# Wider moving operands in two of the three product groups of a split-precision attention kernel

## The chip, the cores and the metric

The kernel runs on one core of one Trainium2 chip. A time is the device time of one execution in microseconds (us). Ten executions of the kernel before the change lie between 2486.03 and 2490.31 us, with a median of 2488.53 us. A profile is taken from one more execution: it records the start and the duration of every instruction on TensorE (matmuls as PE, weight loads as PEld), VectorE (DVE), ScalarE (ACT), GpSimd (POOL) and SyncE (SP), and of every DMA packet.

## The reference

For each of four images, x has 4096 positions (64 x 64) with 256 channels. Cut to what matters:

```python
q = jnp.einsum('bwhc,cd->bwhd', x, Wq) + bq      # 128 channels
k = jnp.einsum('bwhc,cd->bwhd', x, Wk) + bk      # 128 channels
v = jnp.einsum('bwhc,cd->bwhd', x, Wv) + bv      # 256 channels
pq, pk, pv = q.reshape(B, -1, N), k.reshape(B, -1, N), v.reshape(B, -1, N)   # N = 4096
energy = jnp.einsum('bcn,bcm->bnm', pq, pk)
attention = jax.nn.softmax(energy, axis=-1)
out = jnp.einsum('bcm,bnm->bcn', pv, attention)
return gamma * out.reshape(B, W, H, C) + x
```

So it is a softmax attention over 4096 positions, with a contraction over 128 for the energies and over 4096 for the output. All data is float32.

## The kernel before, in words

**Precision by splitting.** TensorE works here on operands of the type fp32r, a shorter form of float32 that is stored in four bytes. To keep the accuracy of float32, each operand is split into parts: a rounded upper part, and one or two rests. The energies are three products of such parts for each block (line 325): two are accumulated in one PSUM tile, `sa`, and one goes into another, `sb`. ScalarE takes the exponential of both (line 329), VectorE multiplies the two results (`join`, line 339) and so has the unnormalised attention weights x. Then `upper` (line 344, ScalarE) makes h from x, and `halves` (lines 350 and 353, VectorE) makes l and d from x and h.

**The attention products.** `attend` (line 358) multiplies h, l and d with the three parts vh, vl and vd of v. h times vh and l times vl accumulate in the PSUM tiles a0 and a1 (one for each 128 of the 256 output positions of a block, index j); d times vd goes into the tile bb. The result is put together later as (1 + E) times a plus bb (`whole`, line 405).

**The column of ones.** The tiles vh and vl have a pitch of VC = C + 64 = 320 columns for each of the NM = 32 blocks of v: 256 of v, and then 2 that are set to one at the start (line 220); the rest is unused. As h and l are each multiplied with a one in column 256, column 256 of a0 and a1 holds the sum of the attention weights, which is the softmax's denominator. `sums` (line 390) reads that one column, C : C + 1. The second column of ones is read by no one. The products of h and l are so 258 columns wide (`right[:, m, : out_.shape[1]]`, line 378), those of d 256.

**Blocks and order.** An image's output positions are cut into NG = 16 blocks of 256 (g), and the 4096 positions that are summed over into NU = 8 units of 512 (t). One step u is one pair (g, t): 128 steps for an image, 512 in all. The order on every engine is written out by hand (`manual_schedule`, line 200). In each step TensorE gets 12 energy matmuls for the unit three steps ahead (LOOK = 3, lines 523 to 525: two halves k of six matmuls), and then the 24 matmuls of `attend` for this step: eight with h, eight with l, eight with d, in each eight j = 0, 1 outside and i = 0 to 3 inside. Each matmul has a weight load of its own, of 128 x 128. The loops of `attend` before the change are

```python
for left, right in ((h, vh), (l, vl), (d, vd)):
    for j in range(NJ):
        out_ = bb[:, j, :] if left is d else acc[j]
        for i in range(4):
            m = 2 * t + i // 2 + NI * (i % 2)
```

After the last unit of a block ScalarE copies bb out (line 385) and VectorE takes the sums and a0, a1 (lines 390 and 405). The next block's first h product has to wait for that, since a0 and a1 have one buffer each. Other matmuls are those of the projections of q, k and v (lines 136 and 157), and transposes (lines 123, 421, 462). The PSUM tiles a0 and a1 share their places with the projections' tiles of 2 x 256 float32 (line 225), which sets the size of these places.

Of the kernel before, what the change touches and what calls it, by code (L numbers as in the profile page):

```python
# [9 lines left out]
F32 = mybir.dt.float32  # L10
# [10 lines left out]
def kernel(  # L21
# [36 lines left out]
    nc = tc.nc  # L58
    B, W, H, C = x.shape
    P = 128  # L60
    N = W * H
    C2 = C // 2
    NM = N // P
# [23 lines left out]
    ones = const.tile([P, P], F32, name="ones")  # L87
# [111 lines left out]
    with ExitStack() as fast:  # L199
# [12 lines left out]
        ps_o = pool("ps_o", 1, space=PSUM)  # L212
# [3 lines left out]
        vh = qkv.tile([P, NM, VC], F32R, tag="vh", name="vh")  # L216
        vl = qkv.tile([P, NM, VC], F32R, tag="vl", name="vl")
        vd = qkv.tile([P, NM, C], F32R, tag="vd", name="vd")
        for t in (vh, vl):
            nc.scalar.copy(t[:, :, C : C + 2], ones[:, : 2 * NM].rearrange("p (m t) -> p m t", t=2))  # L220

        images, qd, kf, units, loads, now = [], {}, {}, {}, {}, {}

# [134 lines left out]
        def attend(b, u):  # L358

            g, t = divmod(u, NU)  # L360
            if t == 0:
                now["acc"] = [
                    ps_o.tile([P, C + 2], F32, tag=f"a{j}", name=f"a{j}_{b}_{g}")
                    for j in range(NJ)
                ]
                now["bb"] = ps_o.tile([P, NJ, C], F32, tag="bb", name=f"bb_{b}_{g}")
            h, l, d = units[b, u]
            acc, bb = now["acc"], now["bb"]
            for left, right in ((h, vh), (l, vl), (d, vd)):
                for j in range(NJ):  # L370
                    out_ = bb[:, j, :] if left is d else acc[j]
                    for i in range(4):
                        m = 2 * t + i // 2 + NI * (i % 2)

                        nc.tensor.matmul(  # L375
                            out_,
                            left[:, i, j * P : (j + 1) * P],
                            right[:, m, : out_.shape[1]],
                            start=(t == i == 0 and (left is h or left is d and j == 0)),
                            stop=(t == NU - 1 and i == 3 and left is not h),  # L380
                            skip_group_check=True,
                        )
            if t == NU - 1 and (b, g) != (B - 1, NG - 1):
                now["o"] = work.tile([P, NJ, C], F32, tag="o", name=f"o_{b}_{g}")
                nc.scalar.copy(now["o"], bb)  # L385
# [101 lines left out]
        for b in range(B):  # L487
# [20 lines left out]
            for u in range(STEPS):  # L508
                g, t = divmod(u, NU)
# [26 lines left out]
                if u in (1, 3):  # L536
                    halve_v(b, NI - 2 + u // 2)
                attend(b, u)
                if (b, u) == (B - 1, STEPS - 1):
                    finish_last(b, g, loads.pop((b, "x", g)))  # L540
# [13 lines left out]
    with tc.If(nc.values_load(again[0:1, 0:1]) > 0), ExitStack() as general:  # L554
# [7 lines left out]
        ps_o = pool("go", 1, space=PSUM)  # L562
        for b in range(B):
# [16 lines left out]
            for g in range(NG):  # L580
                ps = []
                mx = work.tile([P, 2, NB], F32, tag="mx", name=f"gmx_{b}_{g}")
                for t in range(NP):
# [9 lines left out]
                    p = ppool.tile([P, 2, NB], F32, tag="p", name=f"gp_{b}_{g}_{t}")  # L593
# [7 lines left out]
                for j in range(NJ):  # L601
# [17 lines left out]
                acc = [  # L619
                    ps_o.tile([P, NB], F32, tag=f"o{s}", name=f"go{s}_{b}_{g}")  # L620
                    for s in range(2)
                ]
# [60 lines left out]
```

## Time and profile before

| | before |
|---|---|
| median of 10 runs | 2488.53 us (2486.03 to 2490.31) |
| the profiled execution's own time | 2486.82 us |
| its span, first to last instruction | 2484.9 us |
| granted TensorE clock, mean | 0.999 |
| PE busy / weight loads busy | 2469.5 us (99%) / 2423.3 us (98%), 19982 of each |
| DVE busy / ACT busy / POOL busy | 2103.4 us (85%) / 1805.6 us (73%) / 424.4 us (17%) |
| DMA | 498.92 MB, mean 201 GB/s |

The page gives a group of instructions by its line, engine, operation, tiles and shapes, with how often it ran, its busy time in all, the mean duration of one, and the idle time of the engine just before it. Matmuls are pipelined: the duration of one matmul runs from its start until its last result, and the next one starts long before that. For a stream of matmuls the number that adds up to time is therefore not the duration but the distance from one start to the next. A row of the timeline with "x8" stands for eight matmuls of one kind in a row; the start of the next row less the start of this one, divided by eight, is that distance.

### The profile page before, as it was taken

The page shows a single profiled execution, that of the slowest core. Times are in us where ns is not written, and L with a number is a line of the kernel's source. Part 1 is how long each engine was busy: PE and PEld are TensorE (multiplying, and loading weights), DVE is VectorE, ACT ScalarE, POOL GpSimd, SP SyncE. Part 2 cuts the span into 40 slices and gives each one's busy share as a digit, 9 for nine tenths or more (in the row PEclk, how much of TensorE's full clock was granted, in tenths as well). Part 3 has the DMA queues.
Part 4 walks back from the last instruction along what each step waited for, and adds up shares of the span by engine and source line. Part 5 has one row for each costly group of instructions (what it writes and reads, how often), then busy time and mean ns, then how long its engine had stood idle before and what let it go on. Part 6 is the DMA issues. An engine that isn't in the chain of part 4 may idle for free.

```text
span 2484.9 us, 50133 instructions
## 1 busy us (share of the span) xinstructions
PE 2469.5 (99%) x19982; PEld 2423.3 (98%) x19982; DVE 2103.4 (85%) x2440; ACT 1805.6 (73%) x3138; POOL 424.4 (17%) x780
## 2 busy tenths in 40 slices
PE   9999999999999999999999999999999999999998
PEld 8999999999899999999989999999998999999998
DVE  5888888888688888888869888888886988888887
ACT  5777777776677777777667777777766777777775
POOL 4211111111411111111041111111114111111110
PEclk9999999999999999999999999999999999999999
DMA  7666666664766666666476666666648666666663
GB/s 227 219 199 207 205 202 200 199 209 156 229 211 192 211 208 200 204 191 211 148 241 217 200 193 212 202 208 198 194 150 250 214 201 199 201 204 208 200 195 115
DMA packets 137408, 498.92 MB, mean 201 GB/s; under 512 B 15536, under 2 KB 57264, under 8 KB 137168
## 3 DMA queue, kind: packets, MB, share of 16 engines
q0 software_dynamic: 92320, 453.17, 58.0%
q1 hardware_dynamic: 44304, 42.22, 5.7%
q8 instruction: 160, 2.62, 0.4%
q14 instruction: 80, 0.66, 0.1%
q10 hardware_dynamic: 544, 0.26, 0.0%
HBM read 445.25 MB, written 50.33 MB: 199 GB/s over the span
## 4 chain that ended last, share of the span: by engine, by line


## 5 line engine op out<-in xcount | busy, mean ns | idle before, releaser
L329 ACT ACTIVATE x<-sa 128x512 f32<-128x512 f32 x1024 | 608.3, 594 | 391.6 <-PE sa L325 363.7
L339 DVE TENSOR_TENSOR x<-x,y 128x1024 f32<-128x1024 f32 x512 | 625.4, 1221 | 146.5 <-ACT y L329 146.5
L325 PE MATMUL sa<-q,k 128*128 128x256 f32 x4096 | 740.9, 279 | 1.9 <-ACT x L329 1.8
L350 DVE TENSOR_TENSOR l<-x,h 128x1024 fp32r<-128x1024 f32 x512 | 623.8, 1218 | 3.9 <-DMA kf<-f 3.9
L353 DVE SCALAR_TENSOR_TENSOR d<-h,x 128x1024 fp32r<-128x1024 f32 x512 | 623.8, 1218 | 0.0
L325 PEld LDWEIGHTS sa<-q,k 128*128 128x128 f32 x4096 | 619.3, 188 | 4.1 <-ACT x L329 3.5
L329 ACT ACTIVATE y<-sb 128x512 f32<-128x512 f32 x1024 | 613.9, 600 | 0.0
L375 PE MATMUL a<-vh,h 128*128 128x258 f32 x4096 | 580.7, 284 | 0.0
L375 PE MATMUL a<-vl,l 128*128 128x258 f32 x4096 | 577.6, 284 | 0.0
L344 ACT ACTIVATE h<-x 128x1024 fp32r<-128x1024 f32 x512 | 543.4, 1061 | 45.0 <-DVE x L339 41.0
L325 PE MATMUL sb<-q,k 128*128 128x256 f32 x2048 | 575.0, 281 | 0.0
L375 PE MATMUL bb<-vd,d 128*128 128x256 f32 x4096 | 555.9, 278 | 0.0
L309 POOL DMA_DIRECT2D k<-kf x512 | 279.6, 546 | 1475.0 <-PE sb L325 1456.5
L375 PEld LDWEIGHTS a<-vl,l 128*128 128x128 f32 x4096 | 530.5, 191 | 0.0
L375 PEld LDWEIGHTS a<-vh,h 128*128 128x128 f32 x4096 | 524.8, 190 | 2.1
L375 PEld LDWEIGHTS bb<-vd,d 128*128 128x128 f32 x4096 | 514.2, 189 | 0.0
L325 PEld LDWEIGHTS sb<-q,k 128*128 128x128 f32 x2048 | 384.9, 188 | 10.4 <-ACT y L329 1.7
L136 PE MATMUL qk<-wqk_sb,xts 128*128 128x256 f32 x512 | 121.3, 380 | 0.0
L405 DVE SCALAR_TENSOR_TENSOR o<-a,o 128x256 f32<-128x256 f32 x126 | 47.6, 420 | 86.8 <-ACT o L385 86.8
L157 PE MATMUL v<-xts,wv_sb 128*128 128x256 f32 x512 | 120.3, 379 | 0.0
L157 PEld LDWEIGHTS v<-xts,wv_sb 128*128 128x128 f32 x512 | 97.3, 190 | 13.2
L413 ACT ACTIVATE o<-o,r 128x256 f32<-128x256 f32 x126 | 57.4, 502 | 72.4 <-DVE r L396 72.4
(54 smaller groups left out, 928.0 us busy)
## 6 DMA issues: line engine op xcount, KB each, us to landing
k<-kf POOLq DMA_DIRECT2D x512, 768.0 KB, 4.8
x<-in_x_dram SPq DMA_DIRECT2D x128, 256.0 KB, 3.7
kf<-f POOLq DMA_DIRECT2D x64, 384.0 KB, 3.6
out_dram<-x POOLq DMA_DIRECT2D x63, 256.0 KB, 2.5
qd<-qks POOLq DMA_DIRECT2D x128, 64.0 KB, 2.9
qr<-qd SPq DMA_DIRECT2D x64, 128.0 KB, 5.0
wv_sb<-in_L_conv_Wv_dram POOLq DMA_DIRECT2D x1, 256.0 KB, 7.4
out_dram<-x SPq DMA_DIRECT2D x1, 256.0 KB, 3.9
```

The lines of the kernel that those rows point to most:

```text
L136: nc.tensor.matmul(qk[:, s, :], self.xt[i][:, k, s, :], wqk_sb[:, k, :], start=(k == 0), stop=(k == KC - 1),)
L157: nc.tensor.matmul(vp[:, eh, :], wv_sb[:, k, eh * P : (eh + 1) * P], self.xt[i][:, k].rearrange("p s a -> p (s a)"), start=(k == 0), stop= ...
L309: nc.gpsimd.dma_start(t.rearrange("p (i s) f d -> p i s (f d)", s=2), kf[b, u % NU])
L325: nc.tensor.matmul(to[:, i], kt[:, 2 * k + i, f, :], q[:, f], start=first, stop=last)
L329: nc.scalar.activation(to[:, 2 * k : 2 * k + 2, :], sp.rearrange("p i j d -> p i (j d)"), AF.Exp, scale=scale,)
L339: nc.vector.tensor_tensor(x, x, y, ALU.mult)
L344: nc.scalar.activation(h, units[b, u], AF.Identity, scale=UPPER)
L350: nc.vector.tensor_tensor(l, x, h.bitcast(F32), ALU.subtract)
L353: nc.vector.scalar_tensor_tensor(d, h.bitcast(F32), 1.0 + E, x, ALU.mult, ALU.subtract)
L375: nc.tensor.matmul(out_, left[:, i, j * P : (j + 1) * P], right[:, m, : out_.shape[1]], start=(t == i == 0 and (left is h or left is d and ...
L405: nc.vector.scalar_tensor_tensor(o[:, j, :], a[:, :C], 1.0 + E, o[:, j, :], ALU.mult, ALU.add)
L413: nc.scalar.activation(o[:, j, :], o[:, j, :], AF.Identity, scale=r[:, j : j + 1])
```

## The change

The products of h take 260 columns of vh, those of l take 264 columns of vl, and those of d take 256 as before. Columns 256 to 263 of vh and vl are all set to one at the start, where two columns were set before. The PSUM tiles a0 and a1 get C + 8 columns. The pitch VC of vh and vl stays at 320. Column 256 is read for the sums, as before; the columns behind it are read by no one.

```diff
         for t in (vh, vl):
-            nc.scalar.copy(t[:, :, C : C + 2], ones[:, : 2 * NM].rearrange("p (m t) -> p m t", t=2))
+            nc.scalar.copy(t[:, :, C : C + 8], ones[:, :1].unsqueeze(1).to_broadcast([P, NM, 8]))
...
-                    ps_o.tile([P, C + 2], F32, tag=f"a{j}", name=f"a{j}_{b}_{g}")
+                    ps_o.tile([P, C + 8], F32, tag=f"a{j}", name=f"a{j}_{b}_{g}")
...
-            for left, right in ((h, vh), (l, vl), (d, vd)):
+            for left, right, wide in ((h, vh, C + 4), (l, vl, C + 8), (d, vd, C)):
                 for j in range(NJ):
-                    out_ = bb[:, j, :] if left is d else acc[j]
+                    out_ = bb[:, j, :] if left is d else acc[j][:, :wide]
...
-                            right[:, m, : out_.shape[1]],
+                            right[:, m, :wide],
```

## The prediction

> **What bounds the kernel now.** I read the engines' shares first.
>
> ```profile
> PE   2469.5 (99%) x19982; PEld 2423.3 (98%) x19982; DVE 2103.4 (85%) x2440; ACT 1805.6 (73%) x3138; POOL 424.4 (17%) x780
> ...
> PEclk9999999999999999999999999999999999999999
> ```
>
> TensorE is busy from end to end at its full clock. A share of 99% alone proves little for pipelined matmuls, so the waits come second. This is TensorE's own list of waits, in full:
>
> ```profile
> PE wp L197 <- POOL ident masks.py:199: 2.4, 1, 2.4
> PE sa L325 <- ACT x L329: 1.8, 6, 0.3
> PE xt L123 <- DMA x<-in_x_dram: 1.8, 1, 1.8
> PE ot L462 <- DVE o L457: 1.1, 1, 1.1
> ```
>
> Some 7 us of 2484.9 are waits for others, most of them at the start and the end. The chain of waits on the page is empty, and none is needed: a step lasts as long as its 36 matmuls take to start one after the other. So a change in the distance between starts goes into the time almost one to one. The third view is one step in TensorE's timeline (start, us, kind):
>
> ```profile
> 1016.85 0.39 PE L325 MATMUL sa<-q,k 128*128 128x256 f32 x2
> ...
> 1018.21 1.12 PE L375 MATMUL a<-vh,h 128*128 128x258 f32 x8
> 1019.18 1.13 PE L375 MATMUL a<-vl,l 128*128 128x258 f32 x8
> 1020.14 1.08 PE L375 MATMUL bb<-vd,d 128*128 128x256 f32 x8
> 1021.06 0.39 PE L325 MATMUL sa<-q,k 128*128 128x256 f32 x2
> ```
>
> The 12 energy matmuls take 1018.21 - 1016.85 = 1.36 us, 113 ns each. Eight h products take 0.97 us and eight l products 0.96 us, 120 to 121 ns each. Eight d products, 256 wide like the energies, take 0.92 us, 115 ns each. Two columns more cost 7 ns. That can't be the two columns' own streaming: 113 ns for 256 is 0.44 ns a column at most.
>
> The start times of single matmuls in the trace show it finer (timestamps of 1 ns, averaged over repeats). In 340 of the 512 steps the distances are the same. Energies run at 113.33 ns. Then, from h's first product on, each to the next start: 114.2, 119.2, 125.0, 119.2, 120.0, 123.3, 120.0, 121.7; l's: 118.3, 119.2, 125.0, 119.2, 120.0, 123.3, 120.0, 121.7; d's: 117.5, 116.7, 115.8, 114.2, and 113.3 again. Three things are to be seen. **First**, the first 258-wide product costs 114.2, that is 0.83 ns more than a 256-wide one, or 0.42 ns a column. **Second**, what follows holds a stall over that, 6.67 ns on average (120.83 - 114.17), in a pattern that repeats every eight products. It repeats by its own count and not by i and j: in other steps the 125 falls on another product. **Third**, d's first four products, of 256, still pay 10.8 ns in all. So the stall is a state of the stream, a rhythm that is lost and found again, more than a price of each product. Other rhythms in the trace are 120.00 exactly for 258 (72 steps), and 117.78 for 256 in 67 runs of more than ten energies and d products.
>
> **The change, part by part.** Over all 512 steps the means are 121.4 ns for h (971.6 for eight), 120.7 for l (965.7) and 115.7 for d (925.3). There are 4096 products of each kind.
>
> *Streaming of more columns.* h gets 2 more and l gets 6 more. At 0.42 ns a column from the first-product row that is +0.83 ns x 4096 = +3.4 us for h and +2.5 ns x 4096 = +10.2 us for l, +13.7 us together. Nothing hides this: it is on TensorE.
>
> *The stall.* No product of 260 or 264 columns is in the trace. The bounds for what remains of the 6.67 ns stall are 0 (the first product; the energies) and, above, a stall as now or more. Nearest rows: 4.44 ns for 256 in its second rhythm (117.78 - 113.33), 5.83 ns for 258 at 120.00. 6.67 is the largest steady stall that I find in this trace; a new width shifts the rhythm by another amount per product, and is more likely to land below that than above. I take half, 3.33 ns, for both widths: h would be 113.33 + 4 x 0.42 + 3.33 = 118.3, l 113.33 + 8 x 0.42 + 3.33 = 120.0. Against 120.83 that is -2.5 ns x 4096 = -10.2 us for h and -0.83 ns x 4096 = -3.4 us for l, together -13.6 us. With a stall of 0 it would be -5.8 x 4096 = -23.9 and -4.2 x 4096 = -17.1 us, and d would lose its tail of 10.8 ns x 512 = -5.5 us: -46.5 us. With the stall as now it is +13.7 us. I leave d's tail as it is.
>
> A rule speaks against the change here. The Trainium skill, "TensorE: Matmul & The Clock Gate", section "Back-to-back issue gap", has a warm matmul start N / 2.4 + 2.5 ns after the one before, which estimates 110.0 ns for 258, 110.8 for 260 and 112.5 for 264. By that rule alone the change can only cost, some 13.7 us. The rows say 120.8 for 258 and 113.3 for 256, so something that the rule lacks is at work, and it is larger than what the rule has to say on the added columns.
>
> *The ones.* Two ScalarE copies of 128x64, of 247 and 243 ns at 3.0 us, become 128x256. A ScalarE row of that size and output type takes 420 ns (line 261), so +0.35 us in all. ScalarE then stands idle for 3.04 us until the first transposes are there at 6.45 us; that covers it. Without the cover it would cost 0.35 us.
>
> *Nothing else moves.* The pitch of vh and vl stays 320, so no address in SBUF changes. a0 and a1 keep their places, which the projections' tiles of 2 KB set. `sums` reads the same column. The order of no queue changes.
>
> *What is late next.* If the step of 4.21 us falls to 4.12 (the 46.5 us case), VectorE is next: it is busy for 18.58 us of the stretch from 600 to 620 us, the fuller of the two that I read, which is 3.9 us a step. It stays under TensorE, with little room.
>
> **The sum** is against the profiled execution: 2486.82 - 13.6 = 2473.2 us. The median of the runs is 1.7 us above that execution, so **2475 us** for the median.
>
> **The rivals.**
> (a) *The stall goes almost wholly* because 258 ends on a remainder that the stream can't take in step, and 260 and 264 don't. For it: the first 258-wide product pays nothing, and the period is eight products, in which two columns become sixteen. Against it: a remainder of 4 or 8 in sixteen still shifts. 2488.5 - 46.5 = 2442 us; if only one width profits, about 2455 to 2470.
> (b) *A grid of sixteen columns*: 120.00 less 113.33 is 6.67, sixteen columns at 0.42. If the stream takes 64-byte pieces, 258, 260 and 264 all cost 120.00. The change then doesn't touch the cause. The 440 steps not yet in that rhythm gain 0.83 x 16 ns, 5.9 us; d's eight take 929.6 ns after it and 921.8 in the 340 steps, which takes 3.4 us back. About 2486 us.
> (c) *The other side*: the stall stays as it is, since any width over 256 breaks the step of weight load and matmul, and the added columns stream on top: +13.7 us, 2502 us. For it: 120.83 is just 114.17 plus 6.67, the price of sixteen columns once more, as if one beat were missed per product at any width. It decides as soon as the stall shrinks by less than 1.67 ns, the mean of 0.83 and 2.5.
> (d) *A worse rhythm* than any here, at 125 (the largest distance in the pattern) for both: 4.2 x 8192 = +34 us, 2523 us.
>
> **How the numbers follow.** Forecast, the stall partly gone (2457 to 2483): 0.35. (a): 0.16. (b): 0.13. (c), up to 2512: 0.28. (d): 0.08. About 0.2% (5 us) is what a measurement of this kernel can tell from no change. Faster by more than that: forecast and (a), 0.51. Within: (b), 0.13. Slower: 0.36. The range leaves out (d) and the larger part of (a): 2450 to 2506. Cases of both signs are in it; the likeliest one's own range is 2457 to 2483.
>
> **What would show it.** The start distances in the new trace: h near 118 and l near 120 ns would bear out the forecast, 115.0 and 116.7 rival (a), 120.0 for both (b), 121.7 and 123.3 (c). d's tail tells whether the rhythm is kept: eight d products in 0.91 us, not 0.92. The energies must stay at 113.3, and the waits of TensorE at some 7 us; if they grow, VectorE or ScalarE has become late and the sum is wrong for another reason. It is wrong from the start if the distances of h and l are set by something other than their width.

## The result and the profile after

The changed kernel takes 2497.89 us (median of 8 runs, 2496.82 to 2500.47) against 2488.75 us for the kernel before (28 runs). The ratio is 1.0038, with a 95% interval of 1.0030 to 1.0047: slower by 9 us, where 13.6 us less had been forecast. The profiled execution took 2497.8 us, with a span of 2495.9 us, 11.0 us more than the span before. The engines' shares on its page:

```profile
PE 2480.1 (99%) x19982; PEld 2435.4 (98%) x19982; DVE 2105.0 (84%) x2440; ACT 1806.9 (72%) x3138; POOL 425.7 (17%) x780
```

TensorE's list of waits, in full (who waited, on whom, us in total, times, longest):

```profile
PE wp L197 <- POOL ident masks.py:199: 2.4, 1, 2.4
PE sa L325 <- ACT x L329: 2.0, 7, 0.3
PE xt L123 <- DMA x<-in_x_dram: 1.9, 1, 1.9
PE ot L463 <- DVE o L458: 1.1, 1, 1.1
```

TensorE still waits for others for no more than some 7 us. The list has idle time alone; a gap that the running matmul's own duration of some 280 ns covers is not in it. From the start times, 313 energies before and 310 after have the next start more than 140 ns behind them, some 31 and 30 us over the pace of 113.3 ns, so these gaps did not grow either. No other engine became the bound, and the 11 us are in the products themselves. One step in TensorE's timeline (start, us, kind):

```profile
1026.79 1.12 PE L376 MATMUL a<-vh,h 128*128 128x260 f32 x8
1027.74 1.16 PE L376 MATMUL a<-vl,l 128*128 128x264 f32 x8
1028.73 1.09 PE L376 MATMUL bb<-vd,d 128*128 128x256 f32 x8
1029.66 0.28 PE L325 MATMUL sa<-q,k 128*128 128x256 f32 x1
```

Eight h products take 0.95 us where they took 0.97; eight l products 0.99 where they took 0.96; eight d products, whose width did not change, 0.93 where they took 0.92. The single starts, medians over the 512 steps, each to the next: h 116, 118, 122, 118, 120, 122, 118, 120 ns; l 124, 119, 120, 121, 122, 127, 130, 132; d 115, 119, 120, 118, 118, and then 113. What is to be seen is l: its distances grow to the eighth product.

Added up over all steps from the start times in the two traces, from one matmul's start to the next's:

| us | before | after | change |
|---|---|---|---|
| h | 497.5 | 493.8 | -3.7 |
| l | 494.5 | 509.0 | +14.5 |
| d | 473.8 | 478.1 | +4.3 |
| energies | 732.5 | 728.1 | -4.4 |
| all others | 276.0 | 276.1 | +0.1 |

The energies gain mostly because they run less often in the second pace of 256, the 117.8 ns that the prediction had met: 312 of 6144 have a distance of 116 to 120 ns, 1077 before. At 4.4 ns each that is 3.4 us.

### The profile page after: what moved, and what is told of

It is laid out like the page before. It is cut to its first block, busy times and chain, and to the rows that moved or that the text cites. A ratio compares the mean times of both kernels' runs of the same rounds, so it can differ in the third digit from the quotient of the medians.

```text
span 2495.9 us, 50133 instructions
## 1 busy us (share of the span) xinstructions
PE 2480.1 (99%) x19982; PEld 2435.4 (98%) x19982; DVE 2105.0 (84%) x2440; ACT 1806.9 (72%) x3138; POOL 425.7 (17%) x780
## 4 chain that ended last, share of the span: by engine, by line
## 5 line engine op out<-in xcount | busy, mean ns | idle before, releaser
L376 PE MATMUL a<-vl,l 128*128 128x264 f32 x4096 | 592.2, 287 | 0.0
L376 PE MATMUL a<-vh,h 128*128 128x260 f32 x4096 | 577.3, 283 | 0.0
L376 PEld LDWEIGHTS bb<-vd,d 128*128 128x128 f32 x4096 | 523.8, 189 | 0.0
L157 PE MATMUL v<-xts,wv_sb 128*128 128x256 f32 x512 | 120.3, 379 | 0.0
```

The lines of the kernel that those rows point to most:

```text
L157: nc.tensor.matmul(vp[:, eh, :], wv_sb[:, k, eh * P : (eh + 1) * P], self.xt[i][:, k].rearrange("p s a -> p (s a)"), start=(k == 0), stop= ...
L376: nc.tensor.matmul(out_, left[:, i, j * P : (j + 1) * P], right[:, m, :wide], start=(t == i == 0 and (left is h or left is d and j == 0)), ...
```

## The experiments

Theory 1, from the two traces: each width has its own pace, and 264's is bad. Theory 2: 264 is bad only behind 260. Theory 3: every width over 256 costs the time of 32 columns more than it has, at 0.42 ns a column, rival (c) of the prediction. Ratios are against the kernel before on the same chip, whose median was 2483.35, 2484.93 and 2485.87 us in the three sets of timed runs. The trace of the kernel before belongs to the set with 2488.75 us, so a difference of a few us between a run's trace and that trace need not be the change's. Four programs of products alone were built, each profiled once, with 64 bytes between the moving tile and the weights as the kernel has. The rows of the moving tile have 320 columns as those of vh and vl (384 in the last program), those of the weights 256 as in the kernel in the first program, then 320, 320 and 384. The granted clock is 1.0 in all of the runs below. A column has four bytes; `at` is the column at which the moving operand starts in its row, `shift` that of the weights:

```python
nc.tensor.matmul(out[:, :w], wt[:, i, shift + j*128 : shift + j*128 + 128], mv[:, m, at : at + w], ...)
```

**Streams of one width.**

> Another program, of products alone: runs of 64 products with weights of 128 columns at each of 15 widths from 256 to 320, and of 64 weight columns at six widths, with 24 products of 256 between the runs; no other engine works beside it; its output is not the attention. Theory 1, each width has its own steady pace for a weight load and a product: 256 at 113.3 ns, 258 at 120.0 to 120.9, 260 at 119.5 to 120, 264 at 123 to 125, the same from the eighth product to the last. Theory 2, a grid of sixteen columns: 258 to 272 all at 120.0, 274 to 288 at 126.7. Theory 3, two beats are missed at any width over 256: (width + 32) / 2.4, 121.7 at 260, 123.3 at 264, 126.7 at 272. If the weight load sets the pace, the runs with 64 weight columns go at (width + 16) / 2.4 or less, 114.2 at 258 and 116.7 at 264; if the moving side does, they are as slow as those with 128.

TensorE's timeline; a row of x64 is one width, and its start to the next row's start, divided by 64, is its pace:

```profile
37.98 7.89 PE L58 MATMUL a<-mv,wt 128*128 128x258 f32 x64
45.71 2.89 PE L50 MATMUL sp<-mv,wt 128*128 128x256 f32 x24
48.44 7.84 PE L58 MATMUL a<-mv,wt 128*128 128x260 f32 x64
56.11 2.99 PE L50 MATMUL sp<-mv,wt 128*128 128x256 f32 x24
58.94 8.02 PE L58 MATMUL a<-mv,wt 128*128 128x262 f32 x64
66.80 2.91 PE L50 MATMUL sp<-mv,wt 128*128 128x256 f32 x24
69.54 7.87 PE L58 MATMUL a<-mv,wt 128*128 128x264 f32 x64
77.25 2.91 PE L50 MATMUL sp<-mv,wt 128*128 128x256 f32 x24
```

7.73, 7.67, 7.86 and 7.71 us for 64: 120.8 ns at 258, 119.8 at 260, 122.8 at 262, 120.5 at 264. Over the last 32 products alone, from the start times, the paces are 113.3 (256), 120.8, 120.1 (260), 122.7, 120.0 (264), 123.3 (266), 126.7 (268), 124.5 (270), 123.3 (272) and 133.3 (288). So neither the straight line of theory 3 (121.7, 123.3 and 126.7 at 260, 264 and 272) nor the flat grid of rival (b). And 264 is not slow in the long run: its first products come at 117, 120, 121, 122, 127, 130, 132 and 118 ns, and from the ninth on every one at 120.0. That beginning is the row of l in the changed kernel. No other engine works beside these products, so none is the cause. Theory 1 falls in its own form: what l pays is the **beginning of a run of 264**, and a run of eight is over before the pace is found. Second, the rows of 24 products of 256: after 260 they take 58.94 - 56.11 = 2.83 us, 117.9 each, and after 258 2.73 us, 113.8 each. A run leaves the stream behind it in one pace or the other, and it stays there for all 24. With only 64 weight columns a weight load takes 134 ns in the trace where it took 188 (medians), and the paces are 119.1 (256), 118.7 (258), 120.0 (264) and 124.1 (272): slower at 256, 2 ns faster at 258, the same at 264. A shorter weight load does not take the stall away.

**h and l both 260, both 264, both 256.**

```diff
-            for left, right, wide in ((h, vh, C + 4), (l, vl, C + 8), (d, vd, C)):
+            for left, right, wide in ((h, vh, C + 4), (l, vl, C + 4), (d, vd, C)):   # h260_l260
+            for left, right, wide in ((h, vh, C + 8), (l, vl, C + 8), (d, vd, C)):   # h264_l264
+            for left, right, wide in ((h, vh, C), (l, vl, C), (d, vd, C)):           # h256_l256, sums from ones
```

> h and l both 260 wide. Theory 1 (the price is the width's own): h stays at 964 ns for eight as in the changed kernel, l comes to 955 to 960 in place of 994, d back to some 925 or less: 2478 to 2484 us, faster than 258. Theory 2 (what matters is that h and l have different widths, or how long the off-step run is): l at 960, d as with 258: about 2484. Theory 3 (width + 32 cycles): h and l 121.7, 2495 us.

2493.63 us, ratio 1.0036 (1.0022 to 1.0050). h and l did as theory 1 and 2 said, 963 and 961 ns for eight, and still the kernel is slower: 3303 of the 6144 energies are in the second pace. Theory 1 had expected a time under that of 258. A step:

```profile
1024.75 0.40 PE L325 MATMUL sa<-q,k 128*128 128x256 f32 x2
...
1026.16 1.12 PE L376 MATMUL a<-vh,h 128*128 128x260 f32 x8
1027.12 1.12 PE L376 MATMUL a<-vl,l 128*128 128x260 f32 x8
1028.08 1.07 PE L376 MATMUL bb<-vd,d 128*128 128x256 f32 x8
1028.99 0.39 PE L325 MATMUL sa<-q,k 128*128 128x256 f32 x2
```

Twelve energies take 1.41 us here, 117.5 ns each, without any change to them. In this trace they cost 742.2 us (732.5 before) and d 476.5 (473.8). The 2226 energies more that are in the second pace make up 9.9 us at 4.4 ns each: the loss was moved from the wide products to the narrow ones.

> h and l both 264 wide. Theory 1: h as slow as l, 985 to 995 ns for eight: 2510 to 2515 us. Theory 2 (264 is only slow behind 260): both at 960 to 970: 2485 to 2490. Theory 3: 123.3 ns each, 2509 us.

2498.63 us, ratio 1.0059 (1.0045 to 1.0073). Now it is h that takes 996 ns for eight (118, 120, 121, 123, 127, 130, 132, 118), and l runs at 120.0. So both theories had half: the costly beginning comes once for each run of 264, behind energies of 256 here and behind 260 in the changed kernel. Sixteen of 264 cost less extra than theory 1 had it.

> No column of ones in the products: h and l 256 wide, and the sums are copied from a tile of ones, so the output is not divided by the softmax's denominators. All theories: h, l and d at 113.3 ns, 906 to 910 for eight, so (971.6 + 965.7 + 925.3 - 3 x 908 + waits as before) x 512, some 60 to 70 us less than with 258: 2420 to 2430 us. It is the whole price of the columns over 256. If h, l or d stay above 115 ns, the price is not the width's.

2430.95 us, ratio 0.9788 (0.9773 to 0.9803): 52 us are the whole price of a denominator in the products, of which streaming two columns at 0.42 ns would be 6.8. h took 916.5 ns for eight (with the wait at the start of a block), l 910, d 913. Against the trace before, h, l and d together fell by 63 us, as expected; the energies took 5 us more, as 90 of them have the next start more than 250 ns behind them and not 26.

**One part of the change alone.**

> One part alone: h back at 258, l at 264. If the first seven products of 264 pay for getting into their pace whatever stood before (as in the run of 64 products of 264: 117 to 132 ns, then 120.0), l takes 985 to 995 ns for eight and h 971: 0.5 to 0.8% over the kernel before. If l's price came from following 260, l is at 960 to 966 and the time within 0.2% of before.

2501.60 us, ratio 1.0068 (1.0055 to 1.0082); l 992 ns for eight, h 973, d 936. The price of l did not come from following 260. A step:

```profile
1022.79 1.13 PE L376 MATMUL a<-vh,h 128*128 128x258 f32 x8
1023.76 1.16 PE L376 MATMUL a<-vl,l 128*128 128x264 f32 x8
1024.75 1.10 PE L376 MATMUL bb<-vd,d 128*128 128x256 f32 x8
```

> The other part alone: h at 260, l back at 258. h at 964 ns for eight, l at 960 to 967. If the second pace of 256 (117.8 ns) that follows 260 in the run of products alone decides, d and the energies slow down as in the kernel with 260 for both, unless 258 in between resets it: with the reset 0.1 to 0.3% under the kernel before, without it 0.2 to 0.5% over.

2481.51 us, ratio 0.9989 (0.9980 to 0.9998): h 965 ns, l 966, d 924, and only 398 energies in the second pace. h's part of the change is a gain, small and just clear of no change; l's part is the whole loss.

**The place of the operands.** If the stall is a matter of step and not of columns, something else than the width should move it. Products and weight loads go on side by side: PE was busy for 99% and PEld for 98% of the span before.

> Products alone again, in runs of 64 with 24 products of 256 between; its output is not the attention. Now the widths under 256, the place of the operands and mixed widths. Theory W, the count of columns sets the pace: 256 columns that start 2, 4, 8 or 16 columns into a row of the moving tile go at 113.3 ns as ever, 258 at 120.8 from column 8 or 14 as well, and 258 and 264 keep their 120.8 and 120.0 when the weights start 64, 128 or 192 bytes further. Theory L, pieces of 64 bytes: 256 columns from column 2, 4 or 8 touch 17 pieces and go at 120 or more, from column 16 at 113.3; 258 from column 14 touches 17 and stays at 120.8. Theory B, the two read streams collide in SBUF: the place of the weights moves the pace of 258 and 264 by some ns. Under 256: by width alone (width + 16) / 2.4, 106.7 at 240; if the weight load is the limit, 113.3 at all four. Alternating 258 with 256: if the stall is a lost step that a 256 regains, 114.2 and 113.3, a mean under 115; if not, 117 to 121.

```profile
68.29 7.84 PE L56 MATMUL a<-mv,wt 128*128 128x256 f32 x64
75.97 2.99 PE L48 MATMUL sp<-mv,wt 128*128 128x256 f32 x24
...
99.47 7.82 PE L56 MATMUL a<-mv,wt 128*128 128x256 f32 x64
107.13 2.90 PE L48 MATMUL sp<-mv,wt 128*128 128x256 f32 x24
```

The first pair is 256 columns from column 2, the second 256 from column 16: 7.68 and 7.66 us for 64, **120.0 and 119.7 ns for a width that runs at 113.3 from column 0**. From columns 4 and 8 it is 119.2 and 118.3. 258 from columns 8 and 14 goes at 120.0 and 119.0. Moving the weights by 64, 128 and 192 bytes gives 118.6, 117.8 and 120.0 at 256, 122.2, 118.7 and 120.8 at 258, and 123.3, 120.9 and 120.0 at 264. (The 117.8 is the second pace, in which the products before it already ran, so it need not be the place's.) So theory W falls, as does theory L (column 16 had to be as good as column 0). Theory B stands. Under 256 the paces are 112.1 (240), 116.7 (248), 113.3 (252) and 118.3 (254), no line either. Alternating with 256 helps little: a mean of 117.7 for 258 and 256, no better than the two apart, and 123.3 for 264 and 256, worse than either. Changing the PSUM tile with every product instead of every fourth leaves 258 at 120.8, so the change of tile is not the cause.

**The kernel's own order at 20 places.**

> Products alone, in the kernel's own order: three times eight h products, eight l products and 20 products of 256, then 24 more of 256, with the h and l products' moving operand started 0 to 62 columns into its row of 320 (24 places); the 256-wide ones keep their place. Its output is not the attention. Theory B (the read of the product and the read of the next weights get in each other's way, and their distance in SBUF, taken at 256 bytes, sets how much): the sum of a step of 36 moves with the place, by 10 to 60 ns, and places 64 columns apart (0 and a 64th) would agree; place 16 should be like weights moved by 192 bytes (120.8 for 258 in a long run), 32 like 128 bytes (118.7), 48 like 64 bytes (122.2). Theory W (the count of columns alone): all places alike within 5 ns a step. For 260 and 264 the order 260/258 below 258/258 below 260/264 holds at place 0: about 4200, 4210 and 4240 ns a step; at the other places theory B lets it turn round.

The third step of 36 at 258/258, in ns, by the column at which the wide operand starts: 4208 (0), 4300 (4), 4201 (8), **4180 (12)**, 4270 (16), 4193 (32), 4186 (34), 4246 (48), 4193 (52). 260/264 takes 4240 at 0, **4193 at 16**, 4200 at 32, 4320 at 48. At place 0 the three pairs of widths stand at 4200, 4208 and 4240, as expected; at 16 the order has turned round, and 260/264 is the fastest of the three. Two steps each of 260/264, at 0 and at 16; from x16 to x16 is a step:

```profile
403.45 2.11 PE L58 MATMUL a<-mv,wt 128*128 128x260 f32 x16
...
407.69 2.11 PE L58 MATMUL a<-mv,wt 128*128 128x260 f32 x16
...
418.84 2.08 PE L58 MATMUL a<-mv,wt 128*128 128x260 f32 x16
...
423.03 2.08 PE L58 MATMUL a<-mv,wt 128*128 128x260 f32 x16
```

The third step is not the whole picture. At 2, 16, 20, 40 and 60 the steps of 258/258 take turns, 4270, 4210 and 4270 at 16, as one step leaves the 256-wide products in the one pace and the next in the other; 260/264 at 16 takes 4194, 4192 and 4193 and leads in each. The likeness with moved weights was met within a nanosecond: 120.8, 118.7 and 122.2 ns for 258 were expected at 16, 32 and 48, and the l products take 119.9, 119.3 and 122.0.

**Back in the kernel: the place alone, and the change at another place.** The tiles stay where they are; v and its ones move inside the row's 320 columns, and vd stays where it is. Cut to what matters:

```diff
+    AT = 12
-            nc.scalar.copy(t[:, :, C : C + 2], ...)
+            nc.scalar.copy(t[:, :, AT + C : AT + C + 2], ...)
...
-            h = vh[:, m, :C]
+            h = vh[:, m, AT : AT + C]
...
-                    t[:, m, :C], h.bitcast(F32), -f, v4, ALU.mult, ALU.add
+                    t[:, m, o : o + C], h.bitcast(F32), -f, v4, ALU.mult, ALU.add
...
-                            right[:, m, : out_.shape[1]],
+                            right[:, m, o : o + out_.shape[1]],      # both: o = AT for vh and vl, 0 for vd
```

> The kernel before, 258 for h and l, with v and its ones 12 columns (48 bytes) further into each row of vh and vl. Theory B (the distance in SBUF between the product's operand and the next weights sets the stall): a step of 4180 ns in place of 4206 as in the run of products alone, so -26 ns x 512 = -13 us, ratio 0.994 to 0.996, h and l at about 119.3 ns, d at 913 ns for eight. If the place matters only in a stream without the other engines: ratio 1.000.

2474.05 us, ratio **0.9952** (0.9938 to 0.9965), 12 us less than before with the same columns. This beats both kernels, and is the fastest of the versions timed here that keep the denominators. A step:

```profile
1026.83 1.11 PE L377 MATMUL a<-vh,h 128*128 128x258 f32 x8
1027.78 1.11 PE L377 MATMUL a<-vl,l 128*128 128x258 f32 x8
1028.74 1.08 PE L377 MATMUL bb<-vd,d 128*128 128x256 f32 x8
1029.65 0.39 PE L326 MATMUL sa<-q,k 128*128 128x256 f32 x2
```

> The changed kernel, 260 for h and 264 for l, with v and its ones 16 columns (64 bytes) further into each row. Theory B: a step of 4193 ns in place of 4240, so -47 ns x 512 = -24 us against the changed kernel, and some 7 us under the kernel before (ratio 0.996 to 0.999), with l at 963 and not 994 ns for eight. If what the change costs is the columns: ratio 1.003 to 1.006 as the changed kernel had.

2478.49 us, ratio 0.9970 (0.9958 to 0.9982). These are the widths of the change, and they are faster than the kernel before once v stands 64 bytes further:

```profile
1026.86 1.11 PE L378 MATMUL a<-vh,h 128*128 128x260 f32 x8
1027.81 1.13 PE L378 MATMUL a<-vl,l 128*128 128x264 f32 x8
1028.77 1.08 PE L378 MATMUL bb<-vd,d 128*128 128x256 f32 x8
1029.69 0.39 PE L326 MATMUL sa<-q,k 128*128 128x256 f32 x2
```

l takes 0.96 us where the changed kernel took 0.99 for the same products. Over all steps it is 965 ns for eight against 994.

> The kernel before with v and its ones 4 columns (16 bytes) further. Theory B: a step of 4300 ns in place of 4206, with the 256-wide products left in their second pace of 117.8 ns: up to +94 ns x 512 = +48 us, ratio 1.012 to 1.02; less where a wait at the end of a block sets the stream right again. If the place doesn't matter in the whole kernel: 1.000.

2518.65 us, ratio 1.0132 (1.0117 to 1.0148): the bad place is bad in the kernel too, with 5059 of 6144 energies in the second pace. It is 33 us where up to 48 were expected.

**Both operands moved.**

> Products alone, in runs of 64 with 24 of 256 between, rows of 384 columns; its output is not the attention. The product's operand and the weights are moved by 0 to 64 columns, one of them or both. Theory B as it stands (only the distance of the two counts, at 256 bytes): with both moved by 4, 12, 16, 32 or 48 the paces are those of place 0 (113.3 at 256, 120.8 at 258, 120.0 at 264); operand by 16 equals weights by 48 (120.0 at 256), operand by 32 equals weights by 32 (117.8), operand by 48 equals weights by 16 (118.6); 64 of either equals 0. Rival: each operand's own place against some fixed grid counts; then moving both by 16 is slow too, 118 to 122 at 256. Rival: the order of the 24 products before decides, then 64 of either does not equal 0.

With both moved by 4, 12 or 48 columns 256 runs at 113.3 ns, as at place 0 before; by 16 or 32 at 117.8, which in this program is also the pace at 0. 258 with both moved by 16 or 32 is at 120.8, and 264 with both by 16 at 120.0 with the same costly beginning, two products later. 264 with the operand alone by 16 is at 120.0 from the start, in turns of 123 and 116. 256 with the operand alone by 16 is at 120.0, and with both by 16 at 117.8:

```profile
40.40 7.83 PE L56 MATMUL a<-mv,wt 128*128 128x256 f32 x64
48.07 2.90 PE L48 MATMUL sp<-mv,wt 128*128 128x256 f32 x24
...
122.73 7.70 PE L56 MATMUL a<-mv,wt 128*128 128x256 f32 x64
130.27 2.90 PE L48 MATMUL sp<-mv,wt 128*128 128x256 f32 x24
```

64 columns of either alone give back a pace of place 0: 113.3 for the operand, 117.8 for the weights. So what matters is where the two stand relative to one another, and not a grid of each operand's own: moved together they keep the paces of place 0, and one of them moved by 16 or 48 columns does not. That their distance, counted at 256 bytes, is all that sets the pace is not borne out, though 258 in the kernel's order had met it within a nanosecond. Of four pairs of equal distance in the streams one agrees, 120.0 for the operand by 16 and the weights by 48. Operand by 32 gave 117.8 and weights by 32 113.3, both paces of place 0, where 117.8 was expected of both. Operand by 48 gave 120.1 and weights by 16 118.6; 258 with the operand by 12 gave 118.9 and with the weights by 52, the same distance, 122.1. And 256 at place 0 ran at 113.3 in one program and 117.8 in another, as 258 ran at 120.8 and 120.0, so the state in which a run begins counts as well.

## Why the prediction was wrong, point by point

- **TensorE's start distances set the time:** right. The distances of all matmuls grew by 11.0 us (10.8 by the table's rounded rows), and so did the span; the waits stayed at 7 us. The ones took 403 and some 400 ns where 247 and 243 stood before, and the first copy after them began at 6.46 us and not 6.45: no cost, as said.
- **Added columns at 0.42 ns each:** not borne out as a term of a sum. In a stream that is out of step, 260 and 264 pace at 120.1 and 120.0, under 258's 120.8. The rule of the Trainium skill that was weighed there ("TensorE: Matmul & The Clock Gate", section "Back-to-back issue gap") comes near the result by luck: it makes h dearer by 3.4 us and l by 10.2, and h fell by 3.7 while l rose by 14.5. That section gives the rule for a single isolated matmul, and says that in a stream of pairs of weight load and matmul both set the spacing, which the prediction left out.
- **Half the stall, 3.33 ns, for both widths:** this is the step that failed. For h it gave 118.3 ns; measured 119.3 in the undisturbed steps and 120.6 with the wait at a block's start, so -3.7 us and not -10.2. For l it gave 120.0, and 264's pace in a long run is just that, by luck, since the same half is 1.7 ns short for a long run of 260. But l has runs of eight, and the first seven products of a run pay for getting into step, so that l takes 124.3 on average: +14.5 us and not -3.4. In the terms of the sum, the stall of l is 7.6 ns and that of h 4.3, not 3.33 for both. The prediction had seen that the stall is a state that is lost and found again, and yet priced it as a constant of each product. The sentence that a new width is "more likely to land below" the largest stall in the trace had no row behind it. The two nearest rows that it names, 4.44 and 5.83, both lie above 3.33; put in its place they make the sum -4.6 and +6.8 us, on both sides of nothing. And h was set against 120.83 where its own row, with the 114.2 of the first product, has a mean of 120.3: by its own numbers h would have gained some 8 us and not 10.
- **d's tail left as it is:** it grew by 4.3 us, and the energies, which the sum left out, gained 4.4. With 260 for both widths the energies lost 9.7. Products that the change doesn't touch belong in the sum as soon as the price is a state of the stream.
- **Nothing else moves, and no address in SBUF changes:** true, and it hid what mattered. It took the place for neutral, while the size of the stall depends on it: 256 runs at 113.3 to 120.0 ns by it, and the changed widths at ratio 1.0038 or 0.9970.
- **The rivals:** (c) came nearest in time, 2502, but by luck: its distances, 121.7 and 123.3, are not those measured, and 272 runs at 123.3 and not 126.7. (b) had 120.0 right for long runs of 260 and 264 and fell with 262 and 268. (a) was met by none. (d), 125 for both, is near what l takes, 124.3, and wrong for h. The range of 2450 to 2506 holds the result because it had cases of both signs in it; faster had been the likelier side.

The Trainium skill's "TensorE: Matmul & The Clock Gate", section "Step-by-step: what each phase is for", says that loading the next weights takes no SBUF read bandwidth from the running product, since there are two ports. That would not lead one to expect what the runs show for these operands: moving the weights alone, by 192 bytes, takes 256 from 113.3 to 120.0 ns.

That the two reads wait for one another in SBUF is argued from this, not shown: no run here sees the read itself. Shown are the dependence on the place of the two operands relative to one another, on the width and on the state at the beginning. Why a run of 264 takes seven products to get into step at place 0 stays open.

## What to carry to other kernels

Where matmuls with a weight load each follow one another without a gap, measure the distance of starts, not the duration, and compare it with that of neighbours of another shape: 7 ns for two columns were for the most part a stall, as two columns stream in 0.83 ns. Before trying other widths, try the start of the operand within its row by a few columns; here 12 columns were worth 12 us, and 4 columns cost 33. Price a run by its real length and its whole sequence, the untouched products behind it too, in a program of products alone that repeats the kernel's own order: that program put the place of 12 columns 26 ns a step under place 0, and the kernel showed 12 us over 512 steps, 23 ns each.

## What the runs showed of the hardware that was not expected

- 256-wide products with a weight load each have two steady paces at one and the same place, 113.3 and 117.8 ns, and which one holds depends on the run before: in the first program 117.8 behind 260, and 113.3 behind 258 and 264. 24 products don't end it.
- Narrower is not always faster: 248 columns ran at 116.7 ns, 254 at 118.3 and 256 at 113.3.
- Loading 64 weight columns in place of 128, 134 ns a load and not 188, does not take the stall away: 119.1 ns at 256, and 118.7 in place of 120.8 at 258.
- The rhythm of products alone and that of the whole kernel agree within a nanosecond or two, product by product, where the order is the same, though VectorE and ScalarE are busy for 84% and 72% of the time in the kernel.
